# A four-layer graph network on one core: layer 3's row sums in four column tiles, norm, elu and check steps moved off VectorE, new due times

## The chip, the core and the metric

The kernel runs on one core of a Trainium2 chip (trn2). The metric is the device time of one execution in microseconds (us), the median of the runs. In this text PE is TensorE (matmuls), DVE is VectorE, ACT is ScalarE, POOL is GpSimd and SP is SyncE, whose queue issues the transfers. SBUF and PSUM are the two on-chip memories that tiles lie in; the matmuls of this kernel write tiles called `bank`, which lie in PSUM. The granted clock is the share of full speed at which TensorE's clock ran. The kernel before takes 3436.55 us (3435.45 to 3438.7).

## The reference, cut to what matters

32 graphs of 512 nodes with 256 features go through four layers over one adjacency matrix; each layer's output is added to its input and normalised. All data is float32.

```python
x = _layernorm(x + _L0_gnn_ref(...))   # 8-head attention, layernorm, 256-256-256 MLP, layernorm
x = _layernorm(x + _L1_gnn_ref(...))   # additive (leaky relu) attention, one head
x = _layernorm(x + _L2_gnn_ref(...))   # dot-product attention, relu
x = _layernorm(x + _L3_gnn_ref(...))   # additive attention, 4 heads of 64, elu

# inside layer 3
e = e_src[:, :, None, :] + e_dst[:, None, :, :]
e = jnp.where(e >= 0, e, ALPHA * e)                 # leaky relu
attn = jax.nn.softmax(jnp.where(mask, e, NEG_INF), axis=2)
return jax.nn.elu(jnp.einsum('bijh,bjhd->bihd', attn, q).reshape(B, N, H * D))
```

The kernel leaves the softmax unnormalised, multiplies by the values, computes the row sums with extra matmuls, and divides at the end.

## The kernel before

The kernel plans itself. Every step is handed to a planner with an engine, a guessed duration in ns, and what it reads and writes; `port=True` marks steps that the planner thinks use a port shared by VectorE and GpSimd, and it never lays such steps of the two engines over each other. Up to `WAYS` graphs are in flight, and among steps that can start, the one due first goes first. The result is one fixed order per engine; on the chip the engines follow it in order and wait for each other by semaphores. Parts that matter:

```python
WAYS = 4
PACE = 115.69
TENTHS = (0, 74.36, 86.27, 142.21, ...)         # cut: due times within a graph, by tenths
...
def stats(y, c0, n):                            # mean and inverse deviation of two chunks
    ...                                         # bn_stats, bn_aggr on VectorE
    dve(130, lambda: nc.vector.tensor_scalar_add(rs, mv[..., 1], EPS), [mv], [rs])      # names shortened
    pool(900, lambda: nc.gpsimd.tensor_tensor(rs, rs, mhalf, ALU.pow), [rs], [rs])
    return mv, rs

def normalise(y, dst):
    for c0 in range(0, NC, 2):
        mv, rs = stats(y, c0, 2)
        nm = Slot("rs")
        dve(170, lambda ...: nc.vector.scalar_tensor_tensor(   # the bias step; no port=True
            T(nm)[...], T(mv)[..., 0], -1.0, T(rs)[...], ALU.mult, ALU.mult), [mv, rs], [nm])
        ...                                     # two ScalarE steps: y * rs + nm

# layer 0, after the heads: guard against extreme sums, no port=True
def check():
    r = T(rinv)[:, :NC * H0]
    nc.vector.scalar_tensor_tensor(fit, r, R_MIN, fit, ALU.is_gt, ALU.min)
    nc.vector.scalar_tensor_tensor(fit, r, R_MAX, fit, ALU.is_lt, ALU.min)
dve(370, check, [rinv], [])

# gates (layers 1 and 3), after the projection v
act(220, ...)                                   # gs = exp(0.8 * scores)
plan(PE, 150, ...)                              # turn gs on TensorE, "the turn of the gates"
...                                             # out to memory and back, repeated over partitions

# layer 3, for each head pair k and each chunk pair m0: p holds 2 chunks x 2 heads
for m in range(2):
    for i in range(2):
        h = 2 * k + i
        nc.tensor.matmul(T(sm)[32 * h:32 * h + 32, :], pick[:, 0, :],
                         T(p)[:, 2 * m + i, :], start=(m0 + m == 0), stop=(m0 + m == NC - 1))
```

## Time and profile before

| | before |
|---|---|
| median time | 3436.55 us |
| span of the traced execution | 3432.9 us |
| steady interval between the stores of two graphs | 102.45 us |
| TensorE busy, 600 to 3200 us | 99.5% |
| intervals at the ends | 172.5, 122.5 (first two); 102.5, 76.1, 61.8, 51.2 (last four) |

A row of the groups has the source line, engine, operation, output and inputs, shape, count; then busy us in total and mean ns of one; then the engine's idle time before it and what ended it.

### The profile page before, as it was taken

Reading aid. Unit: us, or ns where it says so; the run is one execution under the profiler, and the core shown is the slowest. Engines: PE = TensorE matmul, PEld = TensorE weight load, DVE = VectorE, ACT = ScalarE, POOL = GpSimd, SP = SyncE. Lnnn points to the kernel's source line nnn. Section 1 sums busy time; section 2 is a strip of 40 time slices with the busy share of each in tenths; the row PEclk is TensorE's granted clock in tenths of the full one; section 3 lists DMA queues with packets and bytes.
Section 4 is the critical chain, followed back from the end, with each engine's and each line's share of the span. In section 5 each row is a group of like instructions: output and inputs, shape, how many; then the busy total and the mean of one; then the engine's idle time right before and its main releaser. Section 6 shows DMA issues by size and latency. Waiting matters only on the chain.

```text
span 3432.9 us, 44879 instructions
## 1 busy us (share of the span) xinstructions
PE 3305.5 (96%) x17002; PEld 1735.4 (51%) x17002; DVE 2556.6 (74%) x4970; ACT 1807.7 (53%) x3783; POOL 1029.5 (30%) x811
## 2 busy tenths in 40 slices
PE   8878999999999999999999999999999999999985
PEld 3434545555545555545555545555555555555543
DVE  4456787777887777887777787777787777787774
ACT  4335455555555555555555555555555555455532
POOL 0233232233332233332233332333333233333221
PEclk9889999999999999999999999999999999999998
DMA  2000000000000000000000000000000000000000
GB/s 79 4 13 16 16 29 28 29 4 25 29 28 29 28 4 25 29 28 29 28 6 23 29 28 29 29 16 13 28 28 29 29 23 9 25 28 29 22 22 26
DMA packets 49087, 83.43 MB, mean 24 GB/s; under 512 B 3808, under 2 KB 39776, under 8 KB 44768
## 3 DMA queue, kind: packets, MB, share of 16 engines
q1 hardware_dynamic: 44864, 76.88, 6.8%
q10 hardware_dynamic: 4000, 3.61, 0.3%
q8 instruction: 135, 2.21, 0.3%
q14 instruction: 88, 0.72, 0.1%
HBM read 63.38 MB, written 17.10 MB: 23 GB/s over the span
## 4 chain that ended last, share of the span: by engine, by line
PE 59%; DVE 23%; ACT 4%; issue 1%; DMA 0%; POOL 0%; POOLq 0%; SPq 0%; DVEq 0%; ACTq 0%
PE bank L860 8%; DVE p L1177 6%; PE bank L949 6%; DVE p L1184 6%; PE bank L1154 6%; PE bank L1193 5%; PE bank L1200 5%; PE bank L1095 5%; PE bank L979 5%; PE bank L982 4%; PE bank L1025 3%; PE bank L1013 3%; PE bank L846 3%; PE bank L833 3%; DVE st L874 2%; DVE p L971 2%
## 5 line engine op out<-in xcount | busy, mean ns | idle before, releaser
L879 POOL TENSOR_TENSOR rs<-rs,mhalf 128x2 f32<-128x2 f32 x384 | 408.9, 1065 | 1487.9 <-DVE rs L877 1482.3
L971 DVE TENSOR_TENSOR p<-p,edge_t 128x2048 f32<-128x2048 f32 x256 | 590.6, 2308 | 89.7 <-ACT p L953 81.4
L953 ACT ACTIVATE p<-bank 128x512 f32<-128x512 f32 x1024 | 540.6, 601 | 188.5 <-PE bank L949 186.1
L821 ACT ACTIVATE t<-bank 128x512 f32<-128x512 f32 x640 | 374.0, 595 | 498.3 <-PE bank L846 305.0
L874 DVE BATCH_NORM_STATS2 st<-y 128x6 f32<-128x256 f32 x768 | 316.2, 412 | 245.8 <-POOL v L1082 150.4
L891 ACT ACTIVATE x<-y,rs,rs 128x256 f32<-128x256 f32 x512 | 281.5, 593 | 377.8 <-DVE rs L887 290.2
L899 POOL TENSOR_TENSOR y<-y,x 128x512 f32<-128x512 f32 x192 | 245.2, 1284 | 678.1 <-DVE far L1054 211.6
L1177 DVE TENSOR_SCALAR p<-p,e,e 128x512 f32<-128x512 f32 x512 | 313.3, 651 | 15.2 <-DMA p<-row 15.2
L1184 DVE TENSOR_TENSOR p<-p,edge_t 128x2048 f32<-128x2048 f32 x128 | 321.0, 2508 | 4.3
L949 PE MATMUL bank<-t,t 32*128 32x512 f32 x2048 | 296.5, 641 | 0.0
L979 PE MATMUL bank<-p,v 128*32 128x512 f32 x2048 | 275.7, 609 | 15.8 <-DVE p L971 15.7
L1193 PE MATMUL bank<-p,v 128*64 128x512 f32 x1024 | 252.9, 615 | 26.5 <-DVE p L1184 26.5
L821 ACT ACTIVATE v<-bank 128x258 f32<-128x258 f32 (+2 forms) x384 | 175.0, 467 | 183.9 <-PE bank L860 177.3
L982 PE MATMUL bank<-p,pick 128*32 128x512 f32 x2048 | 269.3, 596 | 0.0
L1095 PE MATMUL bank<-v,p 128*128 128x257 f32 x1024 | 255.1, 395 | 11.3 <-DVE p L1089 10.6
L1095 PEld LDWEIGHTS bank<-v,p 128*128 128x128 f32 x1024 | 187.1, 191 | 122.3 <-issue 100.3
L1200 PE MATMUL bank<-p,pick 128*32 128x512 f32 x1024 | 245.6, 601 | 0.0
L846 PE MATMUL bank<-t,wqkv_sb 128*128 128x512 f32 x512 | 240.2, 594 | 0.7 <-ACT t L821 0.7
L1120 PE MATMUL bank<-t,t 128*128 128x512 f32 x512 | 234.1, 592 | 0.0
L1154 PE MATMUL bank<-v,p 128*128 128x256 f32 x1024 | 233.6, 382 | 0.0
L1154 PEld LDWEIGHTS bank<-v,p 128*128 128x128 f32 x1024 | 192.0, 190 | 48.8 <-issue 24.0
L833 PE MATMUL bank<-ident,x 128*128 128x128 f32 x1024 | 160.1, 283 | 23.8 <-ACT x L891 23.4
(113 smaller groups left out, 4591.7 us busy)
## 6 DMA issues: line engine op xcount, KB each, us to landing
p<-row SPq DMA_DIRECT2D x32, 1024.0 KB, 4.7
x<-in_x_dram SPq DMA_DIRECT2D x32, 512.0 KB, 4.8
out_dram<-x SPq DMA_DIRECT2D x32, 512.0 KB, 3.1
e<-row SPq DMA_DIRECT2D x32, 256.0 KB, 3.1
e<-in_adj_dram SPq DMA_DIRECT2D x4, 256.0 KB, 4.6
wqkv_sb<-in_L_gnn_w_qkv_dram ACTq DMA_DIRECT2D x1, 768.0 KB
y<-in_L_gnn_W_dram ACTq DMA_DIRECT2D x2, 256.0 KB
row<-gT SPq DMA_DIRECT2D x32, 2.0 KB
```

Source lines behind the costliest of these rows:

```text
L821: act(170 + n * 0.84, lambda: nc.scalar.activation(to(T(dst)), frm(T(src)), AF.Copy), [src], writes)
L879: pool(900, lambda: nc.gpsimd.tensor_tensor(T(rs)[:, c0:c0 + n], T(rs)[:, c0:c0 + n], mhalf[:, :n], ALU.pow), [rs], [rs])
L949: nc.tensor.matmul(T(banks[j]), T(kT)[r, g, m * P:(m + 1) * P], T(qT)[r, g, :], start=True, stop=True)
L953: act(600, lambda j=j: nc.scalar.activation(T(p)[:, j, :], T(banks[j]), AF.Exp, scale=1.0 / math.sqrt(D0)), [banks[j]], [(p, j)])
L971: dve(2300, lambda p=p, m=m: nc.vector.tensor_tensor(T(p), T(p), edge_t[:, m, :].unsqueeze(1).to_broadcast([P, J, N]), ALU.mult), [p], [p] ...
L979: nc.tensor.matmul(T(av)[r, :], T(v)[:, m, h * D0:(h + 1) * D0], T(p)[:, j, :], start=(m == 0), stop=(m == NC - 1))
L1095: nc.tensor.matmul(T(bank)[:, :C + 1], T(p)[:, m, c * P:(c + 1) * P], T(v)[:, m, 2:C + 3], start=(m == 0), stop=(m == NC - 1))
L1154: nc.tensor.matmul(T(bank)[:, j * C:(j + 1) * C], T(pT)[:, m, c * P:(c + 1) * P], T(v)[:, m, :C], start=(m == 0), stop=(m == NC - 1))
L1177: nc.vector.tensor_scalar(T(p)[:, 2 * m + i, :], T(G)[:, h, :], T(e1)[:, r:r + 1], T(e02)[:, r:r + 1], ALU.mult, ALU.max)
L1184: nc.vector.tensor_tensor(p4, p4, edge_t[:, m0:m0 + 2, :].unsqueeze(2).to_broadcast([P, 2, 2, N]), ALU.mult)
L1193: nc.tensor.matmul(T(av)[i * D3:(i + 1) * D3, :], T(q)[:, m0 + m, 2 * H3 + h * D3:2 * H3 + (h + 1) * D3], T(p)[:, 2 * m + i, :], start=(m0 ...
L1200: nc.tensor.matmul(T(sm)[32 * h:32 * h + 32, :], pick[:, 0, :], T(p)[:, 2 * m + i, :], start=(m0 + m == 0), stop=(m0 + m == NC - 1))
```

## The change

Its intent: fewer TensorE cycles (four column tiles run side by side instead of two), a lighter VectorE, and a better filled start and end. The core of the diff (cuts marked with "..."):

```diff
-WAYS = 4
-PACE = 115.69
-TENTHS = (0, 74.36, 86.27, 142.21, ...)
+WAYS = 5
+PACE = 96.59
+TENTHS = (0, 19.61, 28.13, 116.86, ...)
...
-        dve(130, lambda: nc.vector.tensor_scalar_add(
+        pool(250, lambda: nc.gpsimd.tensor_scalar_add(
             T(rs)[:, c0:c0 + n], T(mv)[:, c0:c0 + n, 1], EPS), [mv], [rs])
...
+    def rinv3(sm):            # add the even and odd chunks' sums, then the reciprocal
+            nc.vector.tensor_reduce(...)
+            nc.vector.reciprocal(r, r)
... layer 0's second norm: two scalar_tensor_tensor a chunk on VectorE (473 + 485 ns) become
+            normalise_pair(f, f, c0)                                  # ScalarE
+            dve(680, ... nc.vector.tensor_tensor(f, f, g2_row, mult)  # a pair of chunks
+            dve(680, ... nc.vector.tensor_tensor(f, f, xs, add)
... score checks
-            for sign in (1.0, -1.0):
-                nc.vector.scalar_tensor_tensor(seen, wide, sign, seen, ALU.mult, ALU.max)
+            nc.gpsimd.tensor_tensor(new, wide, wide, ALU.mult)
+            nc.gpsimd.tensor_tensor(seen, seen, new, ALU.add)
... layer 3
-                    for m in range(2):
-                        for i in range(2):
-                            h = 2 * k + i
-                            nc.tensor.matmul(T(sm)[32 * h:32 * h + 32, :], pick[:, 0, :], ...)
-                plan(PE, 3700, run, [q, p], [av, sm])
+                    for j in range(4):
+                        nc.tensor.matmul(T(sm)[32 * j:32 * j + 32, :], pick[:, k, :],
+                                         T(p)[:, j, :], start=(k == 0 and m0 == 0),
+                                         stop=(k == KC - 1 and m0 == NC - 2))
+                plan(PE, 2800, run, [q, p], [av, sm])
... elu: the minimum on VectorE becomes a Relu on ScalarE
```

There is now a bias step for layer 0's second norm too: 12 a graph instead of 10.

## The prediction

> **What bounds the kernel now.** I read first the page's busy shares and its forty slices, then a table of four stretches, then the timelines of the steady middle, then TensorE's waits near the start.
>
> ```profile
> PE 3305.5 (96%) x17002; PEld 1735.4 (51%) x17002; DVE 2556.6 (74%) x4970; ACT 1807.7 (53%) x3783; POOL 1029.5 (30%) x811
> ...
> PE   8878999999999999999999999999999999999985
> ...
> PEclk9889999999999999999999999999999999999998
> ```
>
> TensorE is the only engine near full; its gaps and its lowered clock lie in the first slices and the last. Busy time of a matmul is modelled, so I checked by stretches (columns: the stretch, its length, then busy us and count for PE, PEld, DVE, ACT, POOL, then granted clock, DMA share, GB/s).
>
> ```profile
> 0.00:300.00 300.00, 240.75 (x1230) 118.07 (x1231) 165.79 (x305) 128.24 (x257) 59.20 (x55) 0.91 0.10 32
> 300.00:600.00 300.00, 290.40 (x1490) 160.77 (x1489) 223.72 (x454) 157.75 (x334) 95.46 (x76) 1.00 0.06 21
> 600.00:3200.00 2600.00, 2587.88 (x13400) 1359.19 (x13399) 2008.53 (x3891) 1426.47 (x2988) 824.14 (x636) 1.00 0.07 24
> 3200.00:3433.00 233.00, 186.50 (x888) 97.41 (x886) 158.61 (x322) 95.26 (x206) 50.73 (x46) 0.92 0.07 26
> ```
>
> From 600 to 3200 us TensorE is busy 2587.88/2600 = 99.5%; VectorE 77%, ScalarE 55%, GpSimd 32%. There only TensorE work counts. The queue's timeline shows the rhythm: each of the 32 graphs stores its result 1804.40 - 1701.95 = 102.45 us after the one before.
>
> ```profile
> 1701.95 0.39 SPq L1229 DMA_DIRECT2D out_dram<-x  x1
> ...
> 1804.40 0.39 SPq L1229 DMA_DIRECT2D out_dram<-x  x1
> ```
>
> Two pieces of TensorE's timeline follow. I use steps from start to start, which need no modelled end. One record is half of an fp32 matmul, so x8 is four matmuls.
>
> ```profile
> 1704.79 1.06 PE L979 MATMUL bank<-p,v 128*32 128x512 f32 x8
> 1705.67 1.04 PE L982 MATMUL bank<-p,pick 128*32 128x512 f32 x8
> 1706.64 2.00 PE L1095 MATMUL bank<-v,p 128*128 128x257 f32 x8
> ```
>
> ```profile
> 1743.17 1.94 PE L1193 MATMUL bank<-p,v 128*64 128x512 f32 x8
> 1745.03 1.91 PE L1200 MATMUL bank<-p,pick 128*32 128x512 f32 x8
> 1746.88 3.72 PE L1025 MATMUL bank<-w_sb,t 128*128 128x256 f32 x16
> ```
>
> Layer 0's row sums (L982) use all four 32-column tiles and take 1706.64 - 1705.67 = 0.97 us for four matmuls; layer 3's (L1200) are the same matmuls in two tiles and take 1746.88 - 1745.03 = 1.85 us. That pair is the whole case for the main part of the change.
>
> **What the Trainium skill says.** "TensorE: Matmul & The Clock Gate", Part 3 (Packing small matmuls), says that matmuls whose outputs start at different 32-partition strips land in different column groups and run concurrently. The trace agrees: 0.97 against 1.85 us. "TensorEngine Tiling (Array Packing)", Key Properties, says that changing the tiling mode drains TensorE. That agrees too: L979, followed by the same mode, steps 0.88 us, L982, followed by another mode, 0.97; so the new sums should cost 0.97, not 0.88. "SBUF — State Buffer", Who interferes with whom, says that GpSimd and certain VectorE operations share a port pair, and that the second to come waits for the whole instruction of the first. The trace before hints at it: GpSimd's 128x512 work of one and the same form has a mean of 1379 ns with g_row and 2272 with bb_row. "GPSIMD Engine Reference", section 3.1, has GpSimd's sum of two fp32 operands at 4497 ns for 2048 elements, 2.2 ns each; here 512 elements take 1284 (y and x), 2.5 each, so it agrees. No small sum or product on GpSimd is in this trace.
>
> **The change, part by part.**
>
> TensorE. Layer 3 issues its sums four times a graph (two head pairs by two chunk pairs), 128 times in all. Medians over the steady part are 1.841 us for L1200 and 0.972 for L982, so a graph loses 4 x (1.841 - 0.972) = 3.48 us. The built programs have the same number of matmuls on TensorE, so nothing is added. I added the median steps of all of a graph's matmuls: 102.36 us, against the 102.45 seen. After: 102.36 - 3.48 = 98.89 (unrounded), and for 32 graphs 3164.5 instead of 3275.6: **-111 us**.
>
> VectorE, hidden in the middle. Rows by shape:
>
> ```profile
> L877 DVE TENSOR_SCALAR rs<-mv 128x2 f32<-128x2 f32 x384 | 67.8, 177 | 10.0
> ...
> L1039 DVE SCALAR_TENSOR_TENSOR y<-y,rs,x 128x256 f32<-128x256 f32 x128 | 62.0, 485 | 8.9
> ...
> L1036 DVE SCALAR_TENSOR_TENSOR y<-y,mv,g_row 128x256 f32<-128x256 f32 x128 | 60.6, 473 | 0.0
> ```
>
> Removed: these 67.8 + 62.0 + 60.6, the elu minimum (L1210, 27.2) and the checks (L1054, 23.0): 240.6 us. Added: 128 products or sums of 128x512 at the 685 ns of L935, 87.7; 64 small bias steps at 178, 11.4; a reduction beside 32 reciprocals, about 4 (estimate): 103. Net -137 us, to about 2420. ScalarE gains 128 normalisations of 128x256 at 590 ns, 75.5, and 64 Relu of 128x512 at 600, 38.4: to about 1922. GpSimd gains 384 small additions and 128 small check steps; an estimate for each is the 105 ns of its smallest memset here plus 2.5 ns an element and some waiting for the port, 0.2 to 0.25 us, so about 115 in all, to 1145. Per graph of 98.9 us this is VectorE 76%, ScalarE 61%, GpSimd 36%: none becomes the bound, and with TensorE full all earlier, this relief is worth nearly nothing in the middle.
>
> Due times. Here the gain is in filling the ends. Setting each matmul's start against the sum of median steps issued before it gives the lost time of the kernel before: 26 us at the first graph's matmul, 100 at 505 us, 102 at 2980, 157 at the end. So the ramp loses 74, the middle 2.5, the tail 55; 26 + 3275.6 + 131 = 3433, the span. The ramp's largest waits are TensorE's for VectorE's masked weights while graph 0 runs nearly alone:
>
> ```profile
> PE bank L1193 <- DVE p L1184: 11.1, 2, 10.8
> PE bank L1095 <- DVE p L1089: 10.6, 2, 9.2
> ```
>
> I laid the two built programs' matmul orders side by side. Before, graph 0's layers 1, 2 and 3 end after 108, 136 and 156 us of TensorE work, but in the trace near 149, 187 and 229 us: there was not enough other work between them. After, they end after 133, 171 and 226 us of work, since graph 1's layer 0 now ends at 93 instead of 162; plus the 26 us start that is 159, 197 and 252 us, later than the graph's own latency needs. From there on the graphs end 97 to 99 us of work apart at once, where before the first intervals were 171 and 118. I put the ramp's loss at **20 instead of 74**. In the tail, the last graph's layer 3 is alone in both: from its layer 2's end, near 3369, to 3433 are 64 us with 20 of work, 44 lost; after, about 43. Graph 30's layer 3 now lies between graph 31's layer 2 matmuls, so the earlier 11 may shrink to 8: **tail 51 instead of 55**.
>
> Sum: 26 + 3164.5 + 20 + 3 + 51 = 3264.5 span, plus the 3.65 by which the median time exceeds the traced span: **3268 us**, -4.9%.
>
> **The rivals.** (1) Only the four tiles pay; the ramp stays as it was: 3268 + 54 = 3322. For it: the order assumes model durations that I cannot check; against: the order itself does fill the gaps. (2) A new wait in the middle: more work on GpSimd, in order, behind VectorE's long masked products (2.3 us each) on the shared port, and five graphs on the same buffers. Each percent that TensorE idles there costs 32 us; two percent, with the new ramp, gives about 3330. For it: the power step already waits for VectorE 1482 us in total; against: the middle ran at 99.5% with just such schedules, and GpSimd stays under 40%. (3) The four tiles don't overlap as L982's do, because the even and odd chunks' weights come with two different columns of the picker: the middle keeps 102.4 and the time is 3268 + 111 = 3379. Against: L982 does exactly this. (4) Everything fills better, ramp 10 and tail 45: 3252.
>
> **Range and chances.** The four tiles are nearly sure (give or take 5 us), the ramp give or take 18, the tail 10, a loss in the middle 0 to 30. Hence 3235 to 3310. Faster by 2% means under 3368, which even rival 1 and 2 meet: 0.97; same 0.025; slower 0.005.
>
> **What would show it.** The sums' step should be 0.97 us in place of 1.84; the stores 98.9 us apart from the second graph on; TensorE 99% or more busy in the middle; the first 300 us with over 265 us busy in place of 241 and fewer stretches of lowered clock; VectorE's sum near 2420, ScalarE's 1922, GpSimd's 1145. It is wrong if the stores lie over 100 us apart, if TensorE waits in the middle for GpSimd or VectorE, or if the first store comes after 330 us.

## More of the kernel before

From the groups by shape of the kernel before, small VectorE steps:

```profile
L994 DVE SCALAR_TENSOR_TENSOR fit<-ri,fit 128x32 f32<-128x32 f32 x32 | 38.1, 1192 | 1.1
...
L993 DVE SCALAR_TENSOR_TENSOR fit<-ri,fit 128x32 f32<-128x32 f32 x32 | 26.5, 827 | 0.0
...
L1054 DVE SCALAR_TENSOR_TENSOR far<-v,far 128x32 f32<-128x32 f32 x64 | 12.0, 188 | 16.8 <-ACT v L821 15.6
```

All three are the same operation on 128x32, with two tiles in SBUF as inputs. One takes 188 ns, the other two 827 and 1192. The planner allows 370 for the pair. So the kernel before already shows small VectorE steps that take four to six times their own length; in its order nobody waited for them. A count over its trace says when: all 64 of the long ones begin while a GpSimd addition (L899) runs and end with one, and 127 of the 128 steps of L1054 begin while GpSimd does nothing.

## The result

The changed kernel takes 3352.11 us (3351.77 to 3352.51); the kernel before, 3437.3 us in the same rounds. Ratios here and below are the mean time of one kernel's fast runs over that of the other's in the same rounds, so not quite the ratio of the quoted medians: 0.9753, with a 95% interval of 0.9736 to 0.9769. It is faster, but by 2.5% instead of the 4.9% forecast, and 3352 lies outside the range of 3235 to 3310.

The page of the changed kernel, in the lines that answer to those of before:

```profile
PE 3218.1 (96%) x17002; PEld 1707.5 (51%) x17002; DVE 2459.2 (73%) x4362; ACT 1900.6 (57%) x3975; POOL 1219.9 (36%) x1323
...
PE   8999999999999999999999999999999999999985
...
PEclk9999999999999999999999999999999999999998
```

The start is full now. What the slices can't show is the middle, so here are the same four stretches of the changed kernel (columns as before: busy us and count for PE, PEld, DVE, ACT, POOL, granted clock, DMA share, GB/s):

```profile
0.00:300.00 300.00, 280.72 (x1512) 145.03 (x1513) 193.76 (x344) 164.59 (x333) 81.84 (x98) 0.99 0.11 34
300.00:600.00 300.00, 294.00 (x1569) 155.10 (x1568) 225.64 (x396) 175.47 (x368) 115.08 (x123) 0.99 0.07 25
600.00:3100.00 2500.00, 2448.06 (x13018) 1297.39 (x13020) 1878.31 (x3294) 1451.39 (x3041) 958.72 (x1013) 0.99 0.07 24
3100.00:3350.00 250.00, 195.32 (x911) 109.97 (x903) 161.51 (x330) 109.13 (x235) 64.31 (x90) 0.89 0.07 24
```

In the first 300 us TensorE is busy for 281 us instead of 241. In the middle it is busy 2448.06/2500 = 97.9% instead of 99.5, and its clock is 0.99 instead of 1.00. The stores there are 102.05 us apart, with a 100.4 in between now and then: 101.7 on average over the 26 intervals between the first and the last four, where 98.9 had been forecast. One such interval, and the new sums (L1219, the step to the next matmul is 0.99 us):

```profile
1702.11 0.39 SPq L1248 DMA_DIRECT2D out_dram<-x  x1
...
1804.16 0.39 SPq L1248 DMA_DIRECT2D out_dram<-x  x1
```

```profile
1564.58 1.07 PE L1219 MATMUL bank<-p,pick 128*32 128x512 f32 x8
1565.57 1.98 PE L1036 MATMUL bank<-t,w_sb 128*128 128x512 f32 x4
```

In the middle TensorE has one kind of wait left (its waits from 600 to 2900 us, in total, times, longest; all in us):

```profile
PE bank L1080 <- ACT gs L1077: 46.0, 23, 2.0
```

That is 2.0 us once a graph: the turn of layer 3's gates waits for ScalarE's exponential. The timeline of all engines around one such place shows why ScalarE is late (start us, length us, engine, line; in brackets the idle time before and its releaser):

```profile
1636.25 2.50 POOL L903 TENSOR_TENSOR y<-y,x 128x512 f32<-128x512 f32 x2 [2.03 <-DVE y L958]
...
1636.68 0.88 DVE L1016 SCALAR_TENSOR_TENSOR fit<-ri,fit 128x32 f32<-128x32 f32 x1
...
1637.60 1.19 DVE L1017 SCALAR_TENSOR_TENSOR fit<-ri,fit 128x32 f32<-128x32 f32 x1
...
1640.94 1.26 POOL L903 TENSOR_TENSOR x<-x,be_row 128x512 f32<-128x512 f32 x1
1641.00 1.21 DVE L888 SCALAR_TENSOR_TENSOR rs<-mv,rs 128x2 f32<-128x2 f32 x1
...
1642.25 0.60 ACT L892 ACTIVATE y<-y,rs,rs 128x256 f32<-128x256 f32 x1 [2.35 <-DVE rs L888]
1642.76 0.37 ACT L822 ACTIVATE v<-bank 128x264 f32<-128x264 f32 x1
1643.16 0.23 ACT L1077 ACTIVATE gs<-v 128x16 f32<-128x16 f32 x1
...
1643.44 0.28 PE L1080 MATMUL bank<-ident,gs 128*16 128x128 f32 x1 [2.00 <-ACT gs L1077]
...
1643.55 3.42 PE L847 MATMUL bank<-t,wqkv_sb 128*128 128x512 f32 x4
```

Read it from the bottom. The four records of L847 take 3.42 us, where the same four take 1.88 elsewhere: TensorE runs at half speed. Before them it idled 2.00 us for the gates. ScalarE could not copy v out of its bank and take the exponential because, in its fixed order, a normalisation (L892) came first, and that waited 2.35 us for the bias step L888. L888 works on two elements a partition, yet lasts from 1641.00 to 1642.21, exactly until GpSimd's addition of 1640.94 to 1642.20 is over. Further up, the checks L1016 and L1017 end in the same way when each of GpSimd's two additions ends (1636.25 + 2.50 = 1638.75; 1637.60 + 1.19 = 1638.79), and they hold back the statistics behind them. It is so all over this trace: 63 of the 64 checks and 96 of the 384 bias steps last over 0.3 us, and each of these ends within 0.13 us of the end of a GpSimd addition (L903) that was running when it began. "SBUF — State Buffer", Who interferes with whom, says that a VectorE step with two SBUF inputs contends with a GpSimd step that reads SBUF, and that one with at most one SBUF input (outside the two-port modes) does not. The trace looks like the first half; the experiments test both.

The clock shows best in a table of the stretches of 3.4 us around that place (same columns):

```profile
1640.00:1643.70 3.70, 1.70 (x12) 0.57 (x11) 3.56 (x9) 1.30 (x5) 2.78 (x5) 1.00 0.00 0
1643.75:1647.10 3.35, 3.35 (x8) 0.87 (x10) 3.23 (x3) 2.66 (x6) 3.34 (x3) 0.50 0.09 29
```

A stretch of 3.41 us at half clock follows the one with the wait. There are 21 such in 490 to 3100 us, 102.4 us apart or 201.4 where one is left out. "TensorE: Matmul & The Clock Gate", Part 1, describes a free-running window of 3413 ns in which activity is judged; the trace agrees, for 102.4 us are 30 such windows, and a graph that takes 102.05 us slips by 0.35 against them until its wait reaches a border. Then no half-clock stretch comes (five of the 26 times), and that interval is 100.41 us: shorter by 1.64, about half of 3.41.

### The profile page after: what moved, and what is told of

It reads as the page before. It is cut to its first block, busy times and chain, and to the rows that moved or that the text cites. A ratio compares the mean times of both kernels' runs of the same rounds, so it can differ in the third digit from the quotient of the medians.

```text
span 3350.0 us, 45165 instructions
## 1 busy us (share of the span) xinstructions
PE 3218.1 (96%) x17002; PEld 1707.5 (51%) x17002; DVE 2459.2 (73%) x4362; ACT 1900.6 (57%) x3975; POOL 1219.9 (36%) x1323
## 4 chain that ended last, share of the span: by engine, by line
PE 88%; DVE 8%; ACT 1%; POOL 1%; DMA 1%; issue 1%; SPq 0%; DVEq 0%; ACTq 0%; POOLq 0%
PE bank L861 11%; PE bank L847 10%; PE bank L1002 7%; PE bank L972 7%; PE bank L1214 7%; PE bank L1116 7%; PE bank L1141 6%; PE bank L1175 6%; PE bank L1005 6%; PE bank L834 5%; PE bank L1219 4%; PE bank L1048 4%; PE bank L1036 4%; PE bank L955 2%; PE bank L1164 2%; DVE y L958 1%
## 5 line engine op out<-in xcount | busy, mean ns | idle before, releaser
L994 DVE TENSOR_TENSOR p<-p,edge_t 128x2048 f32<-128x2048 f32 x256 | 584.5, 2293 | 224.1 <-ACT p L976 222.1
L878 POOL TENSOR_SCALAR rs<-mv 128x2 f32<-128x2 f32 x384 | 223.9, 583 | 1284.5 <-DVE mv L876 1261.6
L903 POOL TENSOR_TENSOR y<-y,x 128x512 f32<-128x512 f32 x192 | 249.4, 1306 | 640.4 <-ACT y L1180 335.4
L892 ACT ACTIVATE x<-y,rs,rs 128x256 f32<-128x256 f32 x512 | 287.8, 594 | 216.7 <-DVE rs L888 215.9
L880 POOL TENSOR_TENSOR rs<-rs,mhalf 128x2 f32<-128x2 f32 x384 | 348.9, 909 | 29.6
L1198 DVE TENSOR_SCALAR p<-p,e,e 128x512 f32<-128x512 f32 x512 | 287.2, 619 | 18.7 <-DMA p<-row 18.7
L1205 DVE TENSOR_TENSOR p<-p,edge_t 128x2048 f32<-128x2048 f32 x128 | 293.5, 2293 | 4.4
L847 PE MATMUL bank<-t,wqkv_sb 128*128 128x512 f32 x512 | 268.8, 653 | 0.0
L1005 PE MATMUL bank<-p,pick 128*32 128x512 f32 x2048 | 266.6, 592 | 0.0
L1116 PE MATMUL bank<-v,p 128*128 128x257 f32 x1024 | 232.1, 386 | 7.2 <-DVE p L1110 7.2
L892 ACT ACTIVATE y<-y,rs,rs 128x256 f32<-128x256 f32 x256 | 143.6, 604 | 129.1 <-DVE rs L888 129.1
L888 DVE SCALAR_TENSOR_TENSOR rs<-mv,rs 128x2 f32<-128x2 f32 x384 | 157.9, 411 | 78.6 <-POOL rs L880 75.9
L1175 PEld LDWEIGHTS bank<-v,p 128*128 128x128 f32 x1024 | 189.6, 190 | 49.7 <-ACT y L1180 22.0
```

What stands on the lines that cost most here:

```text
L847: nc.tensor.matmul(T(bank), w[:, i, col:col + P], T(xT)[:, i, :], start=(i == 0), stop=(i == KC - 1))
L892: act(590, lambda c=c: nc.scalar.activation(T(dst)[:, c, :], T(y)[:, c, :], AF.Identity, bias=T(nm)[:, c:c + 1], scale=T(rs)[:, c:c + 1]), ...
L994: dve(2300, lambda p=p, m=m: nc.vector.tensor_tensor(T(p), T(p), edge_t[:, m, :].unsqueeze(1).to_broadcast([P, J, N]), ALU.mult), [p], [p] ...
L1005: nc.tensor.matmul(T(sm)[j * 32:(j + 1) * 32, :], pick[:, g, :], T(p)[:, j, :], start=(g == 0 and m == 0), stop=(g == KC - 1 and m == NC - 1))
L1116: nc.tensor.matmul(T(bank)[:, :C + 1], T(p)[:, m, c * P:(c + 1) * P], T(v)[:, m, 2:C + 3], start=(m == 0), stop=(m == NC - 1))
L1175: nc.tensor.matmul(T(bank)[:, j * C:(j + 1) * C], T(pT)[:, m, c * P:(c + 1) * P], T(v)[:, m, :C], start=(m == 0), stop=(m == NC - 1))
```

## The experiments

Two theories were set against each other. **Hold-ups:** VectorE's small steps with two SBUF inputs are held up by GpSimd's additions; ScalarE, then TensorE, gets late by 2 us a graph, and the idle stretch costs half a window of clock besides. **Load:** with TensorE 3.5 us shorter a graph, something else is simply the bound (ScalarE, VectorE, the five graphs in flight). All runs gave the right outputs. Unless said otherwise, an edit leaves the order of the steps as it was. Eleven kernels ran.

### Only the four tiles

The kernel before with the four tiles and the reduction; planner durations untouched (3700), so the order is that of before.

```diff
-    nc.tensor.matmul(T(sm)[32 * h:32 * h + 32, :], pick[:, 0, :], T(p)[:, 2 * m + i, :], ...)
+    nc.tensor.matmul(T(sm)[32 * j:32 * j + 32, :], pick[:, k, :], T(p)[:, j, :], ...)
```

> The kernel before with one thing changed: layer 3's row sums in four column tiles (and the small reduction that goes with them); due times, order of all instructions and everything else as before. Theory (TensorE is the bound, and in the old order nothing else comes close): the whole saving of 128 x 0.87 = 111 us arrives, stores 99.0 us apart, time about 3326 us, so faster than the changed kernel as it stands (3352). Rival (the saving is lost wherever it is made, because VectorE or the order takes over as the bound): stores over 100.5 us apart, time 3370 or more.

Measured: 3360.35 us, ratio 0.9779 (0.9763 to 0.9796). The stores are 99.92 us apart, 2.53 less than before, not 3.48. In the middle TensorE now waits 1.1 us a graph for a normalisation on ScalarE. There VectorE works without a pause through steps ordered for the longer row sums, and the bias step comes late in its queue. So the tiles alone gave 76 of 111 us: most of the saving arrives. That the fixed order, laid out for other durations, takes the rest is how the trace reads; no run with only a new order tests it. Neither theory's number was met: at this place the bias step itself takes its usual 0.15 us, so it is load in an old order and not a hold-up.

### Without the checks

The two checks of layer 0 left out (a wrong kernel as a guard; the outputs stay right on these inputs).

```diff
-            nc.vector.scalar_tensor_tensor(fit, r, R_MIN, fit, ALU.is_gt, ALU.min)
-            nc.vector.scalar_tensor_tensor(fit, r, R_MAX, fit, ALU.is_lt, ALU.min)
```

> The changed kernel without the two small VectorE checks of layer 0's reciprocals (wrong on purpose as a guard only: the outputs stay the same on these inputs), order otherwise unchanged. Theory (in the middle TensorE waits 2.0 us a graph for a ScalarE step that sits behind a normalisation, which is late because small VectorE steps with two SBUF inputs were held up by 1.27 us GpSimd additions; these checks take 0.88 + 1.19 us there): about 2 us of the delay goes, TensorE's wait before the layer 3 turn of the gates falls from 2.0 to under 0.6 us, the half-clock windows in the middle go, stores about 99 us apart, time 3275 to 3290. Rival (the wait has another cause, such as ScalarE's own load): wait 2.0 us and time 3345 to 3355 as now.

Measured: 3280.06 us, ratio 0.9546 (0.953 to 0.9562). The time is as the theory had it; TensorE's wait is 0.85 us instead of the under 0.6 expected, no half-clock stretch is left in the middle, and the stores are 99.3 us apart. Two small steps a graph, of 0.18 us each when free, cost the changed kernel 72 us.

### The bias step on GpSimd

Two GpSimd steps right behind the power in place of the VectorE step.

```diff
+            nc.gpsimd.tensor_scalar_mul(nm, mv[..., 0], -1.0)
+            nc.gpsimd.tensor_tensor(nm, nm, rs, ALU.mult)
-        dve(170, lambda: nc.vector.scalar_tensor_tensor(nm, mv[..., 0], -1.0, rs, ...))
+        dve(170, lambda: None, [mv, rs], [nm])
```

> The changed kernel with the small bias step of the normalisation (mean times inverse deviation, 128x2) moved from VectorE to GpSimd, right behind the power, as two GpSimd steps; order otherwise unchanged. Theory: the step that took 1.21 us instead of 0.15 on VectorE in the late chain takes about 0.45 on GpSimd, so TensorE's wait falls from 2.0 to about 1.3 us, and with a shorter idle stretch fewer or no half-clock windows are left: 3295 to 3335. Rival (the hold-up of that step is not on the chain): unchanged or, with more work on GpSimd, slower: 3350 or more.

Measured: 3344.49 us, ratio 0.9732 (0.9716 to 0.9748): outside what the theory expected. The wait before the gates only fell to 1.67 us, and another of 1.2 us a graph appeared (a transpose waiting for a normalisation). The two new GpSimd steps take 692 and 407 ns on average, not the 0.2 or so expected: they wait for VectorE's steps in their turn (123 of the 384 of the first kind last over 0.3 us, and each ends with a VectorE step that was running when it began). The cost had changed sides. One thing is clear all the same: no half-clock stretch is left in the middle. In this place a wait of 2.00 us brought them, one of 1.67 did not; "Telling the planner" shows that this is no general threshold.

### Filling the wait

Two needless matmuls ahead of layer 3's turn of the gates; the turn itself waits as before.

```diff
+            if heads == H3:
+                for k in range(2):
+                    nc.tensor.matmul(T(bank), ident, wqkv_sb[:, k, 0:N], start=True, stop=True)
             nc.tensor.transpose(T(bank)[:R, :P], T(gs)[:, :R], ident)
```

> The changed kernel with two needless matmuls of 128x512 (about 1.75 us of TensorE work whose result is overwritten) ahead of layer 3's turn of the gates, where TensorE idles 2.0 us a graph. Theory (the half-clock windows of 3.41 us, one in nearly every graph of the middle, come from that idle stretch): the time of the wait itself stays lost, but TensorE no longer idles, the half-clock windows in the middle go, the stores are all about 100.4 us apart, time about 3352 - 26 x 1.7 + a few us in ramp and tail, where there was no wait to fill: 3308 to 3325. Rival (the lowered clock has another cause, such as the transposes or a fixed rhythm): windows as now, time 3350 or more.

Measured: 3314.35 us, ratio 0.9643 (0.9627 to 0.9659). From the table of stretches of this run:

```profile
600.00:3000.00 2400.00, 2397.72 (x12752) 1269.85 (x12744) 1824.24 (x3209) 1417.74 (x2965) 930.20 (x984) 1.00 0.07 24
```

The clock is 1.00 throughout, and every interval is 100.42 us. More work on TensorE made the kernel 38 us faster. So the half-clock stretches come from the idle time, and the loss in the middle splits in two: 101.7 - 100.4 = 1.3 us a graph is clock, and the rest is the wait itself.

### The checks read PSUM

The same checks in the same place, now on the sums in PSUM with the limits turned round: one SBUF input instead of two. (A few steps near the end changed places, because a bank is held longer.)

```diff
-            nc.vector.scalar_tensor_tensor(fit, r, R_MIN, fit, ALU.is_gt, ALU.min)
-            nc.vector.scalar_tensor_tensor(fit, r, R_MAX, fit, ALU.is_lt, ALU.min)
+            s = T(sums).rearrange("p (q r) -> p r q", r=32)[:, 0:KC, :]
+            f4 = fit.rearrange("p (g q) -> p g q", g=KC)
+            nc.vector.scalar_tensor_tensor(f4, s, 1 / R_MIN, f4, ALU.is_lt, ALU.min)
+            nc.vector.scalar_tensor_tensor(f4, s, 1 / R_MAX, f4, ALU.is_gt, ALU.min)
```

> The changed kernel whose layer 0 checks stay where they are on VectorE, but read the sums in PSUM instead of their reciprocals in SBUF, with the limits turned round, so that each has only one SBUF input; the order is the same but for a few steps near the end. Theory (the checks were held up only because two SBUF inputs meet a GpSimd addition): they take about 0.2 us each instead of 0.86 and 1.19, and the kernel is as fast as without them: TensorE's wait near 0.9 us, no half-clock windows in the middle, 3272 to 3292. Rival (any VectorE work at this place delays the chain, wherever it reads): near 3345.

Measured: 3285.6 us, ratio 0.9562 (0.9546 to 0.9578), nearly what leaving them out gave. The two steps take 180 and 191 ns instead of 861 and 1191. The amount of work and its place are unchanged; only where one operand lies is different. That is the hold-up theory's own test, and the load theory fails it.

### The bias step with one SBUF tensor

```diff
-        dve(170, lambda: nc.vector.scalar_tensor_tensor(nm, mv[..., 0], -1.0, rs, mult, mult))
+            for c in (c0, c0 + 1):
+                nc.vector.tensor_scalar(T(nm)[:, c:c + 1], T(mv)[:, c, 0:1],
+                                        T(rs)[:, c:c + 1], -1.0, ALU.mult, ALU.mult)
```

> The changed kernel with the normalisation's small bias step as two VectorE steps of one element a partition, mean times the inverse deviation given as a per-partition scalar, so that only one SBUF tensor is an input; checks as in the changed kernel, order the same. Theory: the step is no longer held up for 1.06 us by the GpSimd addition beside it (two steps of some 0.13 us), TensorE's wait falls from 2.0 to about 1.0 us, the half-clock windows in the middle go, time 3290 to 3325. Rival (the scalar is read over the same port, or the small step was not on the chain): step still 1.2 us, time 3340 or more.

Measured: 3289.42 us, ratio 0.9574 (0.9558 to 0.959), a little better than expected. Each of the 768 steps takes 180 to 217 ns; none is held up any more, not even the 194 that begin while a GpSimd addition runs, though the inverse deviation still lies in SBUF, read as a per-partition scalar. The wait is 1.0 us, and the half-clock stretches are gone.

### Both mends

> Both of the last two edits. Theory: no small step is held up any more, TensorE's wait before layer 3's turn of the gates goes to near 0, stores 98.4 to 99.0 us apart, time 3255 to 3278, the best so far. Rival (something else ends the wait once the small steps are quick): stores 99.3 or more apart as without the checks, 3278 or more.

Measured: **3256.19 us**, ratio 0.9474 (0.9458 to 0.949). The small steps and the middle, from the groups by shape and the table of stretches of this run:

```profile
L890 DVE TENSOR_SCALAR rs<-mv,rs 128x1 f32<-128x1 f32 x768 | 123.6, 202 | 72.3 <-POOL rs L880 72.0
L1026 DVE SCALAR_TENSOR_TENSOR fit<-bank,fit 128x32 f32<-128x32 f32 x32 | 6.1, 191 | 1.1
L1025 DVE SCALAR_TENSOR_TENSOR fit<-bank,fit 128x32 f32<-128x32 f32 x32 | 5.8, 180 | 0.0
```

```profile
600.00:3000.00 2400.00, 2397.54 (x12907) 1281.95 (x12899) 1834.68 (x3565) 1437.47 (x3021) 964.41 (x1006) 1.00 0.08 25
```

TensorE waits for nothing between 600 and 2900 us, and the stores are 98.34 us apart. This is the best version of all: a complete kernel, with all its checks. It also closes the account: the 27 intervals before the last four add up to 2745.3 us in the changed kernel and to 2653.5 here, 92 us less, and the traced spans differ by 3350.0 - 3255.1 = 95.

### Telling the planner

The changed kernel, with the bias step and the checks marked `port=True` and nothing else; a new order follows.

```diff
-            ALU.mult, ALU.mult), [mv, rs], [nm])
+            ALU.mult, ALU.mult), [mv, rs], [nm], True)
-        dve(370, check, [rinv], [])
+        dve(370, check, [rinv], [], True)
```

> The changed kernel with nothing changed but what its own planner believes: the bias step and the checks are marked as users of the shared port, as the larger two-input steps are, so the planner lays them beside GpSimd's work no more; the order of all engines is new and the due times are not tuned to it. Theory (the loss comes from hold-ups that the planner did not see): with them seen, the middle loses less: stores 99 to 100.5 us apart, time 3270 to 3325. Rival (the due times are tuned to this one order and any new order is worse): 3340 or more.

Measured: 3344.63 us, ratio 0.9737 (0.9721 to 0.9754), so the rival's number. The known waits in the middle are small now, but the stores come in pairs, 81 and 120 us apart, 100.4 on average, with 9 half-clock stretches from 600 to 2900 us and a longer end. The checks still take 1042 and 722 ns on average: 48 of the 64 still meet a GpSimd addition on the chip. So the mark did not keep them apart, and this run does not test the hold-up theory; whether due times tuned anew would help was not run. It does correct a reading of the clock: eight of the nine half-clock stretches follow a window of 3.41 us in which TensorE idled only 1.1 to 1.5 us in all (by the modelled ends of matmuls). So the length of an idle stretch does not decide alone; what else counts stays open.

### The rest without the four tiles

The kernel with both mends, with the row sums in two tiles again.

```diff
-                        nc.tensor.matmul(T(sm)[32 * j:32 * j + 32, :], pick[:, k, :], T(p)[:, j, :], ...)
+                            j = 2 * k + i
+                            nc.tensor.matmul(T(sm)[32 * j:32 * j + 32, :], pick[:, 0, :], T(p)[:, 2 * m + i, :], ...)
```

> The last kernel with both hold-ups mended (3256 us), but with layer 3's row sums in two column tiles again, as before; order unchanged. It shows what all the rest of the change is worth without the four tiles, once the hold-ups are gone. Theory (TensorE is the bound in the middle): 4 x 0.87 us come back in each graph, stores 101.8 us apart, time 3256 + 111 = 3360 to 3370, so that the rest alone is worth some 70 us against the kernel before. Rival (the four tiles were partly hidden by other waits, or other engines need the time): 3345 or less.

Measured: 3363.09 us, ratio 0.9787 (0.977 to 0.9803); stores 101.7 us apart, no wait in the middle. Across the two rounds of runs, with the hold-ups gone, the four tiles are worth 3363.09 - 3256.19 = 107 us and all the rest together 3435.41 - 3363.09 = 72.

### The old due times on the mended kernel

```diff
-WAYS = 5
-PACE = 96.59
+WAYS = 4
+PACE = 115.69
```

with the old list of due times.

> The kernel with both hold-ups mended, but with the old due times, pace and four graphs in flight, so a new order. Theory (the due times are worth nothing in the middle and some 70 us at the two ends): first intervals between stores long again (170 and 120 us), the last four again near 290 us in sum instead of 318, middle 98.3 to 99.5, time 3310 to 3340. Rival (the shorter ramp comes from the lighter VectorE work and not from the due times): ramp short, 3250 to 3280.

Measured: 3499.9 us, ratio 1.0179 (1.0162 to 1.0196), 1.8% slower than the kernel before. The first intervals are 168.2, 125.5 and 122.1 us again and the last four sum to 296, so the ends follow the due times, with the pace and the number of graphs in flight, and not the lighter VectorE, as the theory had it. But the middle fell apart (104.8 us apart, 21 half-clock stretches), which no theory had expected.

### The four tiles and the new due times on the old steps

The kernel before with the four tiles (planned at 2800) and the new due times; norm, elu and checks as before.

```diff
-WAYS = 4
-PACE = 115.69
+WAYS = 5
+PACE = 96.59
```

with the new list of due times.

> The kernel before with the four tiles and the new due times, pace and five graphs in flight, but with norm, elu and checks left on VectorE as before. Theory (the new due times fill the ramp by themselves, and VectorE's 137 us of extra work stay hidden beside a full TensorE): ramp short (second and third interval near 100 us), middle 99 to 101 us, time 3270 to 3330. Rival (with the old VectorE work the new order starves TensorE): middle over 102, time 3350 or more.

Measured: 5289.01 us, ratio 1.5396 (1.537 to 1.5421). This is the rival's side, and far beyond its number. The stores are 170.7 us apart, and TensorE waits for normalisations and masked weights nearly everywhere, with a mean clock of 0.851. The due times belong to one set of steps and don't carry over. Why the planner's order is quite so bad here was not pursued.

## Why the prediction was wrong, and where it was right

The prediction took the span apart into five terms. By its own method (a matmul's start against the median steps issued before it), they came out so:

| term | predicted us | changed kernel us |
|---|---|---|
| start | 26 | 28 |
| TensorE work of 32 graphs | 3164.5 | 3164.5 (taken as given) |
| ramp, to about 500 us | 20 | 12 |
| middle, to 3090 us | 3 | 75 |
| tail | 51 | 70 |
| span | 3264.5 | 3350.0 |

The stated range was also narrower than its own terms: all of them at their worst give 3268 + 63 = 3331, and not 3310. The measured time lies beyond that too.

- **The tiles: right.** The new sums step 1565.57 - 1564.58 = 0.99 us (L1219 to the next matmul) where 0.97 was forecast, and two tiles against four are worth 107 us in the mended kernel where 111 was forecast.
- **The ramp: right, a little low.** The first 300 us have 281 us of TensorE work ("over 265"), and the first interval between stores is 100.2 us instead of 172.5. The run with the old due times has the long ramp back.
- **The engine sums: near for two.** VectorE 2459 (2420), ScalarE 1901 (1922). For VectorE this is partly luck: the bias steps took 158 us where 68 were reckoned (56.8 + 11.4), and other steps came out lower. GpSimd is at 1220 and not 1145: its 384 small additions take 583 ns on average against 0.2 to 0.25 expected, waits for the port included, while its power steps fell from 409 to 349 us.
- **The middle: wrong, and this decides.** The step that failed is "the middle 2.5", carried over as 3 from the kernel before. A loss of up to 30 us was allowed for; 75 came, and with stores over 100 us apart the prediction's own sign of being wrong. Rival 2 named the right port and, with its two percent, the right idle time, but the wrong victim: it had GpSimd waiting behind VectorE's long products. What delays TensorE is the reverse: VectorE's steps of 2 and 32 elements wait for GpSimd's additions of 1.27 us. It hits 2.0 us of TensorE's time in each graph, and 1.3 more through the clock, which no step of the prediction had. The sign was there to be read: two 128x32 rows at 827 and 1192 ns beside one of 188. With the two causes taken away and nothing else, the time is 3256, 12 us under the forecast and inside its range. That it comes so near is partly luck: a graph then takes 98.34 us and not 98.89, an estimated 18 us less over 32 graphs, which about makes up for the longer tail.
- **The tail: mis-sized.** 70 us instead of 51. The hold-ups are not the cause: the last four intervals sum to 318.2 us in the changed kernel and to 318.6 in the mended one, against 291.6 before and 296 with the old due times. The new due times buy the short ramp partly with a longer tail. In which steps the 19 us lie was not separated.
- **The relief of VectorE.** "Worth nearly nothing in the middle" nearly fits the run without the four tiles: its stores are 101.7 us apart against 102.45, and its order is new besides. By the stores of the two traces (67 us between the spans), the first two intervals are 93 us shorter, the middle 18, the last four 39 longer, and the first store comes 5 later. That the new due times would work without it is refuted by the last run.

## What to carry to other kernels

Look at rows of tiny steps whose mean is several times that of the same shape elsewhere: they may be held up by another engine, as here, and it costs nothing only until a faster kernel brings someone to wait for them. A planner's order is as good as the contention that it knows, and due times tuned for one set of steps don't fit another. If TensorE must idle for a microsecond or two in a stream of dense work, look for lost clock too (1.64 us a time here), and see whether a step with one SBUF input less ends the wait.

## What the Trainium skill lacked or had wrong

- "TensorE: Matmul & The Clock Gate", in its table "Why this matters for your kernels", advises against idle gaps over some 3 us. Here waits of 2.00 us sufficed: 21 of the 26 steady intervals carry the 1.64 us of a half-clock stretch of 3.41 us. Waits of 1.67 us (bias step on GpSimd) and of 0.85 and 1.0 us brought none, but in "Telling the planner" windows with 1.1 to 1.5 us of idle time in all did. No page says what share of the window must be idle.
- "SBUF — State Buffer", Who interferes with whom, counts SBUF inputs but does not say whether a per-partition scalar operand counts as one; the page on such scalars ("DVE: scalar operands, raw-bit mode, write accounting and state across instructions", section 1) sets them apart from tensor streams but says nothing of the port. Here the scalar does not act as an input: 768 steps with such a scalar took at most 217 ns, where the form with two tensors took up to 1267. Its rule for one SBUF input is borne out: 180 and 191 ns instead of 861 and 1191.
- "GPSIMD Engine Reference", section 3.1, gives times for 512 and 2048 elements only. Here an addition of a constant to 128x2 took 0.22 us when nothing was in its way, and 583 ns on average beside a busy VectorE.
- No page shows how a hold-up at the port looks in a profile: not as a wait, but as a small step with a long busy time, which can stand unseen off the critical path. 64 checks in the kernel before took 64.6 us for about 12 us of work, and cost nothing there.
